# A fused four-block kernel: earlier expert "up" matmuls at the end of block 3, in 19 places that block 3 has left, with pools that wait tile by tile

## The chip, the cores and the metric

The kernel runs on one core of a Trainium2 chip. All data are fp32 apart from the masks. The metric is device time in microseconds (us) for one execution; the median of three runs is taken. The profile is of one execution, with its own time.

Engines: PE is TensorE's matmul and PEld its weight load, DVE is VectorE, ACT is ScalarE, POOL is GpSimd, SP is SyncE, which here issues DMAs.

## The reference

Four blocks follow each other, each on the layer-normalised stream and added back to it:

```python
x = x + L0_attn(layernorm(x))   # block 1: two layers of full attention with an MLP
x = x + L0_ffn(layernorm(x))    # block 2: two layers of windowed attention with a gated MLP
x = x + L1_attn(layernorm(x))   # block 3: windowed and latent attention, mixed by a gate
x = x + L1_ffn(layernorm(x))    # block 4: 64 experts, routed by groups
```

Block 3 has 2 sequences of 1024 positions and width 128, cut into 16 tiles of 128 positions. Its windowed attention has 16 heads of 8 features, its latent attention 4 heads over 64 pooled positions:

```python
local = local_attention(q, k, v)              # window 128
remote = latent(x @ rq, pooled @ rkv) @ rout + rout_b
gate = sigmoid(local @ gl_w + remote @ gr_w)  # per head
out = (gate * local + (1 - gate) * remote) @ out_w + out_b
```

Block 4 computes all 64 experts of 32 hidden features for all 2048 tokens; routing decides what they count for:

```python
scores = softmax(xt @ Wr + br)                # 2048 x 64
# per expert: sort the scores, sum groups of 64 in sorted order,
# keep the best groups over all experts, and mask the scores by them
fs = masked / (masked.sum(-1) + 1e-6)
h = silu(xt @ Wup + bup) * (xt @ Wgate + bgate) * fs[:, :, None]
out = h @ Wdown + fs @ bdown
```

## The kernel before, in words

The blocks run one after another on the core: `stage_a`, `stage_b`, `stage_c`, `stage_d`. In the last two, the order of work on PE, ACT, DVE and POOL is the order in which the program records it (`manual_schedule`), so an instruction waits behind every one that was recorded before it on its engine.

**Block 3 (class `BlockC`).** `prep` (L1139) normalises half a sequence, transposes it to `xT`, and makes queries `qT`, latent queries `rqT`, keys `kT` and values `v`, with a shifted copy `vs`. `score` (L1261), `turn` (L1324), `value` (L1337) and `keep` (L1355) take each tile through scores, softmax, transposed probabilities (`pr`, then `pT`) and values. `latent` (L1395) does the latent attention, `gate` (L1473) the mix of the two and the output projection (transposes L1519, matmuls L1525, added to the stream by `add_tiles`, L517). `both` (L1092) records this in steps; a `Pipe` of "beats" holds work that is due some steps later, and a `beat` records what is due. The last calls of `both`, from L1089, have no new scores to make: they drain what is left. There each step also records two of the sort passes that wait in `front.todo`, unless `self.hold` is set.

**Block 4's front (class `Front`)** runs in those beats too: `tiles` (L1589) normalises a group of finished tiles, transposes it (L1602) into `xTd`, computes router scores (L1608 to L1635), and `turn` (L1643) transposes the scores (L1647) into the layout for sorting, where `sign` (L1657) and sort passes (`sort_pass`, DVE, L1572 and L1573) follow.

**The experts (class `Experts`).** The hidden features are cut into 32 units of two halves each: 64 "up" matmuls (128x128 by 128x512), each followed by a Silu on ACT (L1743) into a place `hid`, and 64 "gate" matmuls of the same size, each multiplied into its `hid`. Most of these products are done by one DVE instruction (L1787); some go through ACT and POOL (L1784, L1785), and eight "late" ones are stored raw by ACT. All these matmuls are line L1734. `up(n)` records n up matmuls and then their n Silus. PSUM tiles are 1024 wide and serve two matmuls each in turn (`bank`, L1082).

Each unit needs a place in SBUF. `new` (L1706) gives them out: the first 10 (`OWN`) in places that block 3 has left, in the pool `own` that outlives it, 19 (`REST`) in a pool of block 4, then two weight tiles, and the last in `xTd` itself, over tokens that every matmul has read by then.

In block 3's end 16 halves are recorded: `up(2)` when the last tile's values are kept (L1390), `up(6)` at the last but one tile's latent output (L1466), `up(2)` after the last gate and `up(2)` three more times in later beats (L1532 to L1534).

**Block 4 (`stage_d`, `route`).** `route` (L1929) runs the remaining sort passes on DVE and, by a running credit, calls `fill` (L1796) between them: one gate product, one more up, and `feed` (L1748), which keeps three gate matmuls ready ahead. When sorted halves have been exchanged by two DMAs (into `r_zab`), a few more passes, group sums (L1981) and a bisection (L2007) follow, then weights for the experts and the down matmuls (L1860) to the output.

PSUM pools (`ps_m`, `ps_c` in block 3, `ps_tr`, `ps_mm`, `ps_d` in block 4) and block 4's SBUF pools (`d1`, `d2`, `dh`) take places that earlier pools have given up. Before, the first use of such a pool waits for all users of the pools whose space it takes.

Of the kernel before, what the change touches and what calls it, by code (L numbers as in the profile page):

```python
# [23 lines left out]
F32 = mybir.dt.float32  # L24
# [5 lines left out]
P = 128  # L30
D = 128
S = 1024
NB = 2
MT = S // P
# [974 lines left out]

def load_c(k, w, I):  # L1010
    nc = k.nc
    k.c_qkv = w.tile([P, 384], F32, name="c_qkv")
    k.c_rq = w.tile([P, 32], F32, name="c_rq")
    k.c_rkv = w.tile([P, 64], F32, name="c_rkv")
    k.c_rout = w.tile([32, D], F32, name="c_rout")
    k.c_out = w.tile([P, D], F32, name="c_out")
    nc.sync.dma_start(k.c_qkv, I["L1_attn_qkv_w"])
    nc.sync.dma_start(k.c_rq, I["L1_attn_rq_w"])
    nc.sync.dma_start(k.c_rkv, I["L1_attn_rkv_w"])
    nc.sync.dma_start(k.c_rout, I["L1_attn_rout_w"])  # L1020
    nc.sync.dma_start(k.c_out, I["L1_attn_out_w"])
# [8 lines left out]
class BlockC:  # L1030
# [61 lines left out]
    def both(self, b=None, m=None, half=None, nxt=None):  # L1092

        on, beat = m is not None, self.pipe.beat
        score, first, second = self.score(b, m, half) if on else [None] * 3
        turn = self.turns and (lambda t=self.turns: self.turn(*t))
        old = self.values
        end, value, keep = [lambda f=f: f(*old) for f in (self.end, self.value, self.keep)] if old else [None] * 3
        if on:
            steps = [[score, end, beat], [beat, value, first], [beat, second, keep], [beat, turn]]  # L1100
        else:
            steps = [[beat, end, value, turn], [beat, keep]]
        for i, now in enumerate(steps):
            for f in now:
                if f:
                    f()
            if nxt and i == 0:
                self.mask(*nxt)
            if not self.hold:
                n = 1 if on else 2  # L1110
                for f in self.front.todo[:n]:
                    f()
                del self.front.todo[:n]
        self.values = self.turns
        self.turns = (b, m, half) if on else None

# [22 lines left out]
    def prep(self, b, j, beats, then=lambda: None):  # L1139
        k, nc, st = self.k, self.k.nc, self.st[b]  # L1140
        t = slice(b * MT + j * 4, b * MT + j * 4 + 4)
        cut = slice(j * 512, (j + 1) * 512)
        new = lambda shape, name: self.p2.tile(shape, F32, tag=name, name=k.name(name))
        if j == 0:
            st["xT"] = self.p1.tile([P, S], F32, tag="xT", name=k.name("xT"))
            st["kT"] = new([P, P + S], "kT")
            for name, rows in (("qT", P), ("rqT", 32)):
                st[name] = self.p5.tile([P, S], F32, tag=name, name=k.name(name))[:rows]
            st["v"], st["vs"] = new([P, MT + 2, 160], "v"), new([P, MT + 1, 160], "vs")
            nc.gpsimd.memset(st["kT"][:, :P], 0.0)  # L1150
            nc.gpsimd.memset(st["v"], 1.0)
            nc.gpsimd.memset(st["vs"][:, 0], 1.0)
# [7 lines left out]
        xT = st["xT"]  # L1160
# [194 lines left out]
    def keep(self, b, m, half):  # L1355
        k, nc, st = self.k, self.k.nc, self.st[b]
        if half == 0:
            st["oT"] = self.p2.tile([P, 2, 4, 64], F32, tag="oT", name=k.name("oT"))
        oT = st["oT"]
        dst, src = oT[:, half].rearrange("p c q -> p (c q)"), st["o"][:, :256]  # L1360
        if self.front.todo or half and (b, m) == (NB - 1, MT - 1):
            nc.scalar.copy(dst, src)
        else:
            nc.vector.tensor_copy(dst, src)  # L1364
        if half == 0:
            return
        local = self.part(b, m, 1, "local")[:, 0, :]
        sel = k.sm("sel", 0, 72).rearrange("p (h n) -> p h n", h=2)

        def rest():  # L1370
            ps = k.bank()
            out = ps[:, :144].rearrange("p (g c d) -> p g c d", c=4, d=9)
            for c in range(4):
                for n in range(2):
                    nc.tensor.matmul(
                        out[n * 64 : n * 64 + 64, :, c, :], oT[:, n, c, :], sel[:, c % 2, :], start=True, stop=True
                    )
            t3 = ps[:, :144].rearrange("p (h d) -> p h d", d=9)
            sums = self.p3.tile([P, 16], F32, tag="sums", name=k.name("sums"))
            nc.vector.reciprocal(sums, t3[:, :, 8])  # L1380
            if m == 0:
                nc.vector.tensor_scalar(sums, sums, k.sm("r1"), None, ALU.mult)
            nc.vector.tensor_tensor(
                local.rearrange("p (h d) -> p h d", d=8), t3[:, :, :8],
                sums[:, :, None].to_broadcast([P, 16, 8]), ALU.mult,
            )
            self.done(b, m)
            if last:
                self.hold = False
                self.ex.up(2)  # L1390

        self.hold = last = (b, m) == (NB - 1, MT - 1)
        self.pipe.later(1 if last else 2, rest, not last, -1 if last else 0)

    def latent(self, b, m):  # L1395
# [55 lines left out]
        def out():  # L1451
            ps = k.bank()
            for u in range(2):
                nc.tensor.matmul(
                    ps[:, u * D : (u + 1) * D], latT[:, u * P : (u + 1) * P], k.c_rout,
                    start=True, stop=True,
                )
            nc.vector.tensor_tensor(
                remote, ps[:, :256].rearrange("p (i d) -> p i d", d=D),
                k.row("c_rout")[:, None, :].to_broadcast([P, 2, D]), ALU.add,  # L1460
            )
            if m == 0:
                self.latent(b, 2)
            self.done(b, m)
            if (b, m) == (NB - 1, MT - 2):
                self.ex.up(6)  # L1466

        self.pipe.chain(
            (1, True, score), (3, False, exp, -1), (2, True, turn), (3, True, value), (2, True, across),
# [3 lines left out]
    def gate(self, b, j):  # L1473
# [48 lines left out]
        def out():  # L1522
            ps = k.bank()
            for i in range(n):
                nc.tensor.matmul(  # L1525
                    ps[:, i * D : (i + 1) * D], mT[:, i * P : (i + 1) * P], k.c_out,
                    start=True, stop=True,
                )
            add_tiles(k, k.xo[:, b * MT + at : b * MT + at + n], ps[:, : n * D])
            self.front.tiles(self, b, at, n)  # L1530
            if last:
                self.ex.up(2)  # L1532
                for beats in (1, 4, 5):
                    self.pipe.later(beats, lambda: self.ex.up(2), False, 1)  # L1534

        beats = (0, 0, 1, 1, 1) if last else (1, 3, 3, 3, 3)
        steps = ((False, products), (False, sums), (False, mix), (True, features), (True, out))
# [151 lines left out]
class Experts:  # L1689
# [1 line left out]

    OWN, REST = 10, 19
    LATE = (26, 29, 32, 35, 58, 60, 62, 64)

    def __init__(self, k, xT, own, wide):
        self.wide = wide
        self.k, self.xT, self.own, self.bank = k, xT, own, None
        self.hid, self.rest, self.raw, self.places = {}, None, {}, []  # L1700
        self.parts = [(tp, h) for tp in range(2) for h in range(NB)]
        self.units = [(tp, h, c) for tp, h in self.parts for c in range(8)]
        halves = [(unit, e) for unit in self.units for e in range(2)]
# [2 lines left out]
    def new(self):  # L1706
        n, k = len(self.hid), self.k
        shape, name = [P, 2, 512], k.name("hid")
        if n < 2 or 8 <= n < self.OWN:
            return self.own.tile(shape, F32, tag=("qT", "rqT")[n % 2], name=name)  # L1710
        if n < self.OWN:
            if n < 6:
                if n % 2 == 0:
                    self.pair = self.own.tile([P, 2048], F32, tag="pr", name=name)
                return self.pair[:, n % 2 * 1024 :][:, :1024].rearrange("p (e t) -> p e t", e=2)
            return self.own.tile(shape, F32, tag="pT", name=name)
        n -= self.OWN
        if n < self.REST:
            return self.rest.tile(shape, F32, tag="hid", name=name)
# [3 lines left out]
        if n == 1:  # L1723
            t = k.wpool.tile([P, NROW], F32, tag="rows", name=name)
            return t[:, :1024].rearrange("p (e t) -> p e t", e=2)

        return self.xT.rearrange("p (b t) -> p b t", b=2)[:, :, :512]

    def matmul(self, unit, e, weights):
# [7 lines left out]
    def up(self, n=1):  # L1737
# [7 lines left out]
            )  # L1745
        del self.ups[:n]

    def feed(self):  # L1748

        while self.gates and len(self.ready) < (3 if self.ups else 4):  # L1750
# [11 lines left out]
    def place(self, k):  # L1762

        if not self.places:
            n, w = len(self.raw), self.wide
            if n == 0:
                t = self.beside.tile([P, 512], F32, name="raw")
            elif n == 1:
                t = w.tile([P, 1024], F32, tag="sc", name="raw_sc")
            elif n == 3:  # L1770
# [25 lines left out]
    def fill(self, n=1):  # L1796


        while n and self.ready:
            now = self.ready.pop(0)  # L1800
            self.gate(*now)
            self.up()
            self.feed()
            n -= not now[0]


def stage_d(k, out, front, ex):
# [2 lines left out]
    nc = k.nc  # L1810
    e = mybir.EngineType
    with ExitStack() as es, k.tc.manual_schedule(engines={e.PE, e.Activation, e.DVE, e.Pool}):
        p1 = es.enter_context(k.tc.tile_pool(name="d1", bufs=1))
        p2 = es.enter_context(k.tc.tile_pool(name="d2", bufs=2))
        ex.rest = es.enter_context(k.tc.tile_pool(name="dh", bufs=ex.REST))
        ex.bank, ex.beside = k.big, p1
        ex.feed()
        fs, rest = route(k, p1, front, ex, ex.fill)
        hid = ex.hid
# [346 lines left out]
def tile_kernel(ctx: ExitStack, tc: tile.TileContext, I, out):  # L2166
    k = K()
# [14 lines left out]
            stage_a(k, b)  # L2182
        stage_b(k, b)
    with ExitStack() as ps:
        psum = lambda n, m: tc.tile_pool(name=n, bufs=m, space=bass.MemoryType.PSUM)
        wcd = ps.enter_context(tc.tile_pool(name="wcd", bufs=1))
        load_d(k, wcd, I)
        front = Front(k, wcd)
# [151 lines left out]
```

## Time and profile before

| | us |
|---|---|
| median of 3 runs (1231.8 to 1233.62) | 1233.22 |
| the profiled execution | 1234.76 |
| its span | 1232.8 |
| PE busy, share of the span | 1091.9 (89%) |
| DVE busy | 866.4 (70%) |
| ACT busy | 618.5 (50%) |
| POOL busy | 483.8 (39%) |

The span lies about so: block 1 to about 330 us, block 2 to 751, block 3 to 985 with its end, in which block 4's front also stands, to 1037, the sort with the experts' matmuls to 1122, and from there bisection, weights and the down matmuls to the end.

How to read the views: a table by stretch gives the busy time of each engine in a stretch of the span, with the TensorE clock that was granted (1.0 is full speed). A list of waits says for each engine and line what ended its idle time, as total, count and longest. The chain that ended last is the work followed back from the last instruction, at each step to what released it. A timeline gives start, duration, engine, line, operation, what is written and read, shape and count, and in square brackets the idle time of the engine before it and what ended it.

### The profile page before, as it was taken

The page shows a single profiled execution, that of the slowest core. Times are in us where ns is not written, and L with a number is a line of the kernel's source. Part 1 is how long each engine was busy: PE and PEld are TensorE (multiplying, and loading weights), DVE is VectorE, ACT ScalarE, POOL GpSimd, SP SyncE. Part 2 cuts the span into 40 slices and gives each one's busy share as a digit, 9 for nine tenths or more (in the row PEclk, how much of TensorE's full clock was granted, in tenths as well). Part 3 has the DMA queues.
Part 4 walks back from the last instruction along what each step waited for, and adds up shares of the span by engine and source line. Part 5 has one row for each costly group of instructions (what it writes and reads, how often), then busy time and mean ns, then how long its engine had stood idle before and what let it go on. Part 6 is the DMA issues. An engine that isn't in the chain of part 4 may idle for free.

```text
span 1232.8 us, 23644 instructions
## 1 busy us (share of the span) xinstructions
PE 1091.9 (89%) x9515; PEld 740.1 (60%) x9547; DVE 866.4 (70%) x1764; ACT 618.5 (50%) x1180; POOL 483.8 (39%) x560
## 2 busy tenths in 40 slices
PE   5999999999778899899899878998999966995799
PEld 2666666665545566666666654665776632442598
DVE  5666675565478767767777743666778999879884
ACT  5555454454355566657556544665666733442100
POOL 1423332224298976766768634222242310200000
PEclk9999999999889999999999988897999988998699
DMA  8100000000011100001000102100000000000000
GB/s 290 34 1 1 1 1 1 1 1 1 1 31 27 23 20 22 23 19 27 19 23 19 23 1 102 27 18 7 2 2 2 2 1 0 1 9 9 1 18 18
DMA packets 23471, 25.56 MB, mean 21 GB/s; under 512 B 6778, under 2 KB 17476, under 8 KB 23108
## 3 DMA queue, kind: packets, MB, share of 16 engines
q1 hardware_dynamic: 23284, 23.81, 7.1%
q8 instruction: 75, 1.23, 0.4%
q10 hardware_dynamic: 80, 0.26, 0.1%
q14 instruction: 32, 0.26, 0.1%
HBM read 13.19 MB, written 1.05 MB: 12 GB/s over the span
## 4 chain that ended last, share of the span: by engine, by line
PE 59%; DVE 26%; ACT 6%; POOL 5%; issue 4%; DMA 0%; DVEq 0%; POOLq 0%; ACTq 0%
PE big L1734 7%; PE bank L410 4%; PE mm L1860 4%; PE s L375 4%; PE bank L965 4%; PE s L730 3%; PE bank L885 3%; DVE r_zab L1572 3%; PE m L1321 3%; PE s L840 2%; PE bank L470 2%; DVE r_zab L1573 2%; PE bank L491 2%; DVE nm L381 2%; PE s L1278 2%
## 5 line engine op out<-in xcount | busy, mean ns | idle before, releaser
L381 DVE TENSOR_REDUCE nm<-s 128x1 f32<-128x1024 f32 x64 | 75.1, 1215 | 51.9 <-PE s L375 51.9
L777 POOL TENSOR_TENSOR t<-raw,tab 128x512 f32<-128x512 f32 x62 | 77.3, 1267 | 74.3 <-DVE raw L768 73.0
L1292 DVE TENSOR_REDUCE nm<-s 128x4 f32<-128x768 f32 x64 | 58.2, 950 | 38.9 <-PE s L1290 33.3
L1734 PE MATMUL big<-xTd,d_gate 128*128 128x512 f32 x128 | 70.6, 646 | 8.6 <-ACT hid L1743 8.0
L739 ACT ACTIVATE sq<-s 128x1024 f32<-128x1024 f32 x32 | 32.8, 1024 | 86.8 <-PE s L730 86.8
L387 ACT ACTIVATE pr<-s,nm 128x1024 f32<-128x1024 f32 x64 | 71.1, 1121 | 7.9 <-DVE nm L381 7.8
L1734 PE MATMUL big<-xTd,d_up 128*128 128x512 f32 x128 | 66.5, 616 | 9.3 <-ACT hid L1743 7.5
L398 PEld LDWEIGHTS bank<-ident,pr 128*128 128x128 f32 x512 | 56.2, 141 | 30.0 <-issue 22.5
L784 POOL TENSOR_TENSOR raw<-raw,tab 128x1024 f32<-128x1024 f32 x31 | 73.2, 2360 | 2.4
L791 POOL TENSOR_TENSOR raw<-raw,t 128x1024 f32<-128x1024 f32 x31 | 73.2, 2362 | 1.7
L410 PE MATMUL bank<-pT,v 128*64 128x128 f32 x1024 | 70.0, 279 | 0.7 <-DVE pT L403 0.2
L401 ACT COPY pT<-bank 128x512 f32<-128x512 f32 x64 | 34.9, 588 | 70.0 <-PE bank L398 70.0
L1743 ACT ACTIVATE hid<-big,cols 128x512 f32<-128x512 f32 x62 | 41.6, 686 | 55.3 <-PE big L1734 55.2
L410 PEld LDWEIGHTS bank<-pT,v 128*64 128x64 f32 x1024 | 55.0, 136 | 22.1 <-issue 10.7
L375 PE MATMUL s<-kk,q 64*128 64x512 f32 x256 | 66.5, 630 | 0.6 <-ACT pr L387 0.5
L398 PE MATMUL bank<-ident,pr 128*128 128x128 f32 x512 | 65.2, 276 | 0.0
L730 PE MATMUL s<-b_wqkv,hT 128*128 128x512 f32 x128 | 63.7, 621 | 1.3 <-ACT hT L697 1.3
L1572 DVE TENSOR_TENSOR r_zab<-r_zab 128x128 f32<-128x128 f32 (+2 forms) x140 | 61.0, 436 | 2.8
L1321 PE MATMUL m<-ident,pr 128*128 128x128 f32 x384 | 58.0, 287 | 5.1 <-DVE oT L1364 2.6
L1573 DVE TENSOR_TENSOR r_zab<-r_zab 128x128 f32<-128x128 f32 (+2 forms) x140 | 55.5, 396 | 0.0
L1860 PE MATMUL mm<-d_down,hid 128*128 128x128 f32 x440 | 53.5, 282 | 0.0
L1860 PEld LDWEIGHTS mm<-d_down,hid 128*128 128x128 f32 x440 | 52.5, 198 | 1.1 <-issue 0.8
(386 smaller groups left out, 2833.8 us busy)
## 6 DMA issues: line engine op xcount, KB each, us to landing
vs<-v SPq DMA_DIRECT2D x60, 130.0 KB, 2.2
b_wqkv<-in_L_ffn_wqkv_dram SPq DMA_DIRECT2D x2, 768.0 KB, 8.9
b_tab<-in_c_xpos_dram SPq DMA_DIRECT2D x1, 1024.0 KB, 9.1
d_up<-in_L_ffn_Wup_dram SPq DMA_DIRECT2D x1, 1024.0 KB
d_gate<-in_L_ffn_Wgate_dram SPq DMA_DIRECT2D x1, 1024.0 KB, 7.0
out_dram<-xo SPq DMA_DIRECT2D x3, 256.0 KB, 2.9
rows<-in_rows_dram SPq DMA_DIRECT2D x1, 760.0 KB, 7.7
vs<-v SPq DMA_DIRECT2D x8, 88.0 KB, 3.6
```

Source lines behind the costliest of these rows:

```text
L375: nc.tensor.matmul(t["s"][h][:, keys], q[rows, qt * P : (qt + 1) * P], kk[rows, keys], start=True, stop=True,)
L381: nc.vector.tensor_reduce(t["nm"][h], t["s"][h], AX.X, ALU.max, negate=True)
L398: nc.tensor.transpose(ps[:, i * P : (i + 1) * P], t["pr", h][:, at : at + P], k.ident)
L410: nc.tensor.matmul(t["u"][h * 64 : h * 64 + 64, :P], v[:, kb, h * 64 : h * 64 + 64], t["pT"][:, h, kb], start=(kb == 0), stop=(kb == MT - 1),)
L730: nc.tensor.matmul(qk[:, cut], lhsT, k.b_wqkv[:, l, cut], start=True, stop=True)
L777: nc.gpsimd.tensor_tensor(t2[:, :, :, a : a + 32], r4[:, :, :, z : z + 32], tab(1)[:, :, None, a : a + 32].to_broadcast([P, 2, 8, 32]), AL ...
L784: nc.gpsimd.tensor_tensor(r4, r4, tab(0)[:, :, None, :].to_broadcast([P, 2, 8, 64]), ALU.mult)
L1321: nc.tensor.transpose(ps[:, c * P : (c + 1) * P], pr[:, c, at : at + P], k.ident)
L1572: nc.vector.tensor_tensor(d[:, :, 0, :], s[:, :, 0, :], far, ALU.max)
L1573: nc.vector.tensor_tensor(d[:, :, 1, :], s[:, :, 0, :], far, ALU.min)
L1734: self.k.nc.tensor.matmul(ps, weights[:, rows], self.xT[:, cut], start=True, stop=True)
L1860: nc.tensor.matmul(sums[part][i], hid[tp, h, c][:, e, cols], k.d_down[:, c + 8 * e, :], start=part == last and c + e == 0, stop=False,)
```

## The change

It has six parts.

1. The five weights of block 3 (`c_qkv`, `c_rq`, `c_rkv`, `c_rout`, `c_out`) become views of one tile `c_w`, whose place later serves the first raw gate product in place of a tile of its own.
2. `prep` takes `xT`, and one tile `kv` for keys, values and shifted values together, from the pool `own`.
3. `OWN` is 19 and `REST` 10: the first 19 units lie where queries, `xT`, `kv` (four units in each), probabilities and transposed probabilities stood.
4. The calls of `up` in `keep`, `latent` and `gate` go. In the draining steps of `both`, `early` records one up (two in the last steps) per step, each matmul with its Silu, until 38 halves are out.
5. `fill` records an up only while more than two are left, and the last two only when half of the gates have been recorded.
6. Block 4's SBUF pools and all PSUM pools of blocks 3 and 4 wait tile by tile (`reuse_waits="tile"`).

```diff
@@ load_c
-    k.c_qkv = w.tile([P, 384], F32, name="c_qkv")
-    k.c_rq = w.tile([P, 32], F32, name="c_rq")
-    k.c_rkv = w.tile([P, 64], F32, name="c_rkv")
-    k.c_rout = w.tile([32, D], F32, name="c_rout")
-    k.c_out = w.tile([P, D], F32, name="c_out")
+    t = w.tile([P, 736], F32, tag="c_w", name="c_w")
+    k.c_qkv, k.c_rq, k.c_rkv = t[:, :384], t[:, 384:416], t[:, 416:480]
+    k.c_rout, k.c_out = t[:32, 480:608], t[:, 608:]
@@ both
                 for f in self.front.todo[:n]:
                     f()
                 del self.front.todo[:n]
+            if not on and not turn:
+                self.ex.early(1 if old or self.hold else 2)
@@ prep
-        new = lambda shape, name: self.p2.tile(shape, F32, tag=name, name=k.name(name))
         if j == 0:
-            st["xT"] = self.p1.tile([P, S], F32, tag="xT", name=k.name("xT"))
-            st["kT"] = new([P, P + S], "kT")
+            st["xT"] = self.p5.tile([P, S], F32, tag="xT", bufs=1, name=k.name("xT"))
+            kv = self.p5.tile([P, 4192], F32, tag="kv", name=k.name("kv"))
+            st["kT"], v, vs = kv[:, : P + S], kv[:, P + S : 2752], kv[:, 2752:]
...
-            st["v"], st["vs"] = new([P, MT + 2, 160], "v"), new([P, MT + 1, 160], "vs")
+            st["v"], st["vs"] = [t.rearrange("p (i d) -> p i d", d=160) for t in (v, vs)]
@@ keep, latent, gate
-                self.ex.up(2)
...
-            if (b, m) == (NB - 1, MT - 2):
-                self.ex.up(6)
...
-            if last:
-                self.ex.up(2)
-                for beats in (1, 4, 5):
-                    self.pipe.later(beats, lambda: self.ex.up(2), False, 1)
@@ Experts
-    OWN, REST = 10, 19
+    OWN, REST = 19, 10
+    PLACES = ("qT", "rqT", "xT", *["kv"] * 4, "qT", "rqT", *["kv"] * 4, *["pr"] * 4, "pT", "pT")
...
-        if n < 2 or 8 <= n < self.OWN:
-            return self.own.tile(shape, F32, tag=("qT", "rqT")[n % 2], name=name)
         if n < self.OWN:
-            if n < 6:
-                if n % 2 == 0:
-                    self.pair = self.own.tile([P, 2048], F32, tag="pr", name=name)
-                return self.pair[:, n % 2 * 1024 :][:, :1024].rearrange("p (e t) -> p e t", e=2)
-            return self.own.tile(shape, F32, tag="pT", name=name)
+            tag = self.PLACES[n]
+            if not self.places_own:
+                size, more = {"kv": (4192, {}), "pr": (2048, {}), "xT": (S, {"bufs": 1})}.get(tag, (S, {}))
+                t = self.own.tile([P, size], F32, tag=tag, name=name, **more)
+                self.places_own = [t[:, i : i + S] for i in range(0, size - S + 1, S)]
+            return self.places_own.pop(0).rearrange("p (e t) -> p e t", e=2)
...
+    def early(self, n):
+
+        for _ in range(n):
+            if len(self.ups) > len(self.gates) - 2 * self.OWN:
+                self.up()
...
-                t = self.beside.tile([P, 512], F32, name="raw")
+                t = self.k.wpool.tile([P, 736], F32, tag="c_w", name="raw_cw")[:, :512]
...
-            self.up()
+            if len(self.ups) > 2 or len(self.gates) <= len(self.units):
+                self.up()
@@ stage_d
-        p1 = es.enter_context(k.tc.tile_pool(name="d1", bufs=1))
-        p2 = es.enter_context(k.tc.tile_pool(name="d2", bufs=2))
-        ex.rest = es.enter_context(k.tc.tile_pool(name="dh", bufs=ex.REST))
-        ex.bank, ex.beside = k.big, p1
+        p1 = es.enter_context(k.tc.tile_pool(name="d1", bufs=1, reuse_waits="tile"))
+        p2 = es.enter_context(k.tc.tile_pool(name="d2", bufs=2, reuse_waits="tile"))
+        ex.rest = es.enter_context(k.tc.tile_pool(name="dh", bufs=ex.REST, reuse_waits="tile"))
+        ex.bank = k.big
@@ tile_kernel
-        psum = lambda n, m: tc.tile_pool(name=n, bufs=m, space=bass.MemoryType.PSUM)
+        psum = lambda n, m: tc.tile_pool(name=n, bufs=m, space=bass.MemoryType.PSUM, reuse_waits="tile")
```

More of the change, by code (lines that the diff above doesn't have):

```diff
@@ L1699, in __init__ @@
         self.k, self.xT, self.own, self.bank = k, xT, own, None
-        self.hid, self.rest, self.raw, self.places = {}, None, {}, []
+        self.hid, self.rest, self.raw, self.places, self.places_own = {}, None, {}, [], []
         self.parts = [(tp, h) for tp in range(2) for h in range(NB)]
@@ L1725, in new @@
             return t[:, :1024].rearrange("p (e t) -> p e t", e=2)
+        assert len(self.gates) <= len(self.units)
         return self.xT.rearrange("p (b t) -> p b t", b=2)[:, :, :512]
```

## The prediction

> **What bounds the kernel now.** I read the page first (PE is busy 89% of the span, DVE 70%), then tables by stretch of the two places that the change touches, block 3's end (985 to 1037 us) and the sort of block 4 (1037 to 1122), then the chain, the waits and the order of work there. In a table by stretch the columns are start:end, length, busy time of PE, PEld, DVE, ACT and POOL (with instructions), granted clock and DMA.
>
> ```profile
> 985.00:995.00 10.00, 8.70 (x48) 5.20 (x48) 9.55 (x29) 3.31 (x6) 0.00 (x0) 1.00 0.00 0
> 995.00:1000.00 5.00, 0.49 (x2) 0.00 (x0) 4.83 (x17) 0.00 (x0) 3.10 (x5) 0.97 0.00 0
> 1000.00:1003.00 3.00, 0.00 (x0) 0.00 (x0) 2.93 (x10) 1.43 (x4) 0.00 (x0) 0.50 0.00 0
> 1020.00:1025.00 5.00, 0.00 (x0) 0.00 (x0) 4.72 (x19) 2.36 (x4) 0.00 (x0) 0.86 0.00 2
> 1040.00:1060.00 20.00, 20.00 (x47) 8.89 (x46) 15.74 (x40) 9.39 (x15) 3.79 (x3) 0.98 0.00 0
> 1080.00:1100.00 20.00, 20.00 (x48) 8.81 (x47) 15.10 (x26) 9.95 (x16) 0.00 (x0) 1.00 0.00 0
> ```
>
> At block 3's end DVE is the bound (9.55 of 10 us) and PE has holes. In the sort it is the reverse: PE is full, DVE has some 4 us free in 20. The chain says so too, and the waits give the size (columns: total, times, longest):
>
> ```profile
> 1037.40 77.42 PE big L1734 x176
> ```
> ```profile
> DVE hid L1787 <- PE big L1734: 14.3, 16, 2.1
> ```
>
> So DVE waits 14.3 us for gate matmuls in the sort: the most that lighter PE work can give there. The matmuls of an up or gate are two records each:
>
> ```profile
> 985.57 1.98 PE L1734 MATMUL big<-xTd,d_up 128*128 128x512 f32 x4
> 990.51 0.71 PE L1525 MATMUL m<-c_out,mT 128*128 128x128 f32 x4 [1.11 <-ACT mT L1520]
> 991.79 3.70 PE L1734 MATMUL big<-xTd,d_up 128*128 128x512 f32 x8
> 1003.00 3.72 PE L1734 MATMUL big<-xTd,d_up 128*128 128x512 f32 x4 [7.51 <-ACT hid L1743]
> 1040.82 1.02 PE L1734 MATMUL big<-xTd,d_gate 128*128 128x512 f32 x2
> 1041.68 1.02 PE L1734 MATMUL big<-xTd,d_up 128*128 128x512 f32 x2
> ```
>
> At full clock one starts every 0.86 us (1040.82, 1041.68); after the idle 7.51 us before 1003.00, at clock 0.56, one takes 1.86 (3.72 for two).
>
> **The change part by part.** The built order has the same number of instructions on each engine; SP's and DVE's orders, and all DMAs on SP's queue, are as before. So costs are waits.
>
> *Ups in block 3's end, 16 halves before, 38 after: +8.6 us.* Before, pairs were recorded as two matmuls and then two Silus (L1743). Now each step records one matmul and its Silu. The two halves of a 1024-wide PSUM tile are written by successive ups, and the built order makes the second wait until ACT has read the first. The handoffs come from this row and its neighbours:
>
> ```profile
> 1032.17 0.69 ACT L1743 ACTIVATE hid<-big,cols 128x512 f32<-128x512 f32 x1 [1.71 <-PE big L1734]
> 1032.91 1.12 PE L1734 MATMUL big<-xTd,d_gate 128*128 128x512 f32 x2 [0.86 <-ACT hid L1743]
> ```
>
> An up that ends at 1032.05 (start 1031.03, 1.02 long) is read at 1032.17, Silu takes 0.69, PE goes on 0.05 later. A pair of halves then takes 1.02+0.12+0.69+0.05+0.86 = 2.74 us, against 1.72. Behind every blocked up stands one matmul group of the chain (L1375, L1431, L1519, L1647, L1448, L1525, L1454, L1602, L1608), behind those groups' ACT copies stand DVE's adds: that is the wait added, and DVE, in unchanged order, is who pays. I walked it with the durations of before. The first up starts at 984.4. Silu's table load (1.28) now precedes the copy of oT L1362, so L1375 ends at 989.95, not 985.65, and L1431 at 990.75, not about 988.35; DVE is +2.4 late. Then a pair each 2.74 us puts L1525's first group at 1000.4, not 990.51 (add L517: 1001.2, not 995.03: +6.2), L1454 at 1006.5 (L1458 +7.1), L1525's second at 1017.1, not 1008.61 (L517: 1017.9, not 1009.51: +8.4). From there DVE has no hole left to be hurt: it is busy 4.72 of 5 us, its eight passes cover exp L1629, and r_zab L1657 comes at 1038.3 instead of 1029.58, the first gate L1787 at 1043.6 instead of 1035.01: +8.6. Bounds: +4 if the handoffs cost only up to the first group and the rest fits the holes (PE idles about 21 us of 52 there, the 22 more halves take 22 x 0.86 = 18.9); +12 if each of 22 steps costs 0.55 us in full. I take the walk, since it has the order itself.
>
> [...]
>
> *Clock: -0.8.* Without the holes PE stays warm. Before, the up and gates between 1035.81 and 1040.82 took 5.0 us for work of 3.4 (4 x 0.86) at full clock. Between 0 and -1.7; DVE is partly the one waited for, so half. [...]
>
> *Sort: -8.1 + 0.3 = -7.8.* Of 48 ups 26 remain, two of them at the end. Up to gate 27 ups and gates still alternate at 0.86, three gates in 5.15 us against DVE's 4.35, so the 6.2 us of DVE waits before 1078 stay. After it the gates come alone, 0.86 per matmul, and DVE needs at least 0.67 each plus its passes. These waits go: 0.23, 2.08, 0.48, 1.41, 0.90, 0.97, 1.03, 0.96 = 8.06:
>
> ```profile
> 1083.15 0.75 DVE L1787 SCALAR_TENSOR_TENSOR hid<-big,cols,hid 128x512 f32<-128x512 f32 x1 [2.08 <-PE big L1734]
> 1093.45 0.75 DVE L1787 SCALAR_TENSOR_TENSOR hid<-big,cols,hid 128x512 f32<-128x512 f32 x1 [1.41 <-PE big L1734]
> ```
>
> What is late next is the exchange of halves before L1968. SP's DMA goes out at 1106.39 and lands 2.9 us later; the five gates that hide it take 6.7 us now and 5 x 0.67 = 3.4 then. Its cover nearly gone, it takes back 0 to 0.6, I say 0.3. Ends: -8.1, and -4 if gates behind ACT's set-aside ones or the five single gates still wait half as long.
>
> *Block 3's start: +2.3.* kT, v and vs now share a tile whose place L982's matmuls read, so POOL's first memset waits for the last of them (about 753.7) instead of DVE L971. And POOL's order changes: L993 and the memsets of d_bdown and d_one come before L1159 and the norm. Before:
>
> ```profile
> 751.22 0.20 POOL L1150 MEMSET kT<- 128x128 f32 x1 [10.36 <-DVE hid L971]
> ...
> 759.07 1.26 POOL L993 TENSOR_TENSOR xo<-xo,xi 128x512 f32<-128x512 f32 x1
> ...
> 760.78 2.05 POOL L1255 TENSOR_TENSOR qm<-qT,small_c 128x512 f32<-128x512 f32 x2
> ```
>
> All the same pieces come after the wait: 753.7 + 0.2 + 1.4 + 1.26 (L993) + 0.2 + 0.35 + 1.25 (L1159) + 3.5 (norm) + 1.25 + 1.06 (first qm) = 764.2, against 761.84. The first scores L1278 began at 761.88 after a wait of 1.83 us for just that qm, and everything on PE is queued behind them; PE is then full (20.00 of 20 at 780 to 800). Ends 0 (later holes take it) and +2.5.
>
> *At nothing.* One weight tile c_w with the same DMAs on SP (landed long before use); the place of raw_cw (read last by L1525, 70 us earlier); 19 units in dead places (their last readers, L1349 and the transposes, end by 984.4); one ordering by tile in place of by pool (D's first gate waits for the last Silu alone; DVE is the later one). Each costs 0 to 0.5 if its cover goes.
>
> **Sum** on the profiled execution, 1234.76 us (span 1232.8 and 1.96 around it): 2.3 + 8.6 - 0.8 - 7.8 = +2.3, so 1237.1. The median of the runs, 1233.22, is 1.5 lower; the forecast is 1235.5. Bisect and down (1122 to the end) move with it unchanged.
>
> **Rivals.**
> - *The ups fall into PE's holes* (ends faster). For it: 21 us of holes for 18.9 of work; against: the built waits. Tail 0 to +4: 1233.2 + 2.3 + 2 - 0.8 - 7.8 = 1228.9; it is faster by more than can be told once block 3's end shifts by less than 3.8. Chance 0.25.
> - *Block 3's start is absorbed*: 1235.5 - 2.3 = 1233.2, no change. For it: DVE has free time until 940; against: the serial chain through PE. 0.17.
> - *Handoffs cost in full*: tail +12: 1235.5 + 3.4 = 1238.9. For it: ACT runs Silus and the chain's copies in one order, and table loads (1.28) part them. 0.2.
> - *The sort's waits do not go* (the change doesn't do what it says there): saved 4: 1235.5 + 3.8 = 1239.3. For it: three ready gates and ACT's set-aside ones limit the run ahead; against: the waits named are all for PE. 0.08.
> - The forecast: 0.3.
>
> **How the numbers follow.** The measurement tells 0.2%, 2.5 us, from no change: faster is below 1230.7, slower above 1235.7. Faster: 0.25 from the first rival. Same: 0.17 plus the lower part of the forecast's own range (1232 to 1239), 0.1: 0.27. Slower: the rest, 0.48. The range reaches from the first rival's 1227 (nearly all of its tail hidden) to 1242 (full handoffs and half the waits left, not both in full).
>
> **What would show.** Right: pairs of ups about 2.7 us apart from 984 to 1040; DVE waiting 2 to 4 us for L1525 and L1454; r_zab L1657 some 9 to 11 us later; the waits DVE on PE after gate 27 gone, about 6 us left; first qm at about 764. Wrong: L1657 shifted by under 5 or over 14, PE still full after gate 27, first scores at 762, or DVE waits at new places in the sort.

## The result, and the profile after

The changed kernel takes 1243.18 us (median of five runs, 1237.89 to 1244.49) against 1233.22; the ratio is 1.0077 with a 95% interval of 1.0055 to 1.0100. Its profiled execution took 1243.0 us with a span of 1241.2. It is slower by 10 us, 1.2 us above the upper end of the range.

The sort is where the change works. The chain's stretch of up and gate matmuls was 77.42 us long and is now

```profile
1052.68 54.92 PE big L1728 x126
```

(line L1734 of before is L1728 here). The waits of DVE for these matmuls, 14.3 us before, are in the list of waits of this stretch:

```profile
DVE hid L1787 <- PE big L1728: 4.5, 7, 0.8
```

The stretches of block 3's end and of the sort, as a table (start:end, length, busy time of PE, PEld, DVE, ACT and POOL, granted clock, DMA):

```profile
985.00:995.00 10.00, 7.67 (x95) 4.57 (x94) 7.92 (x23) 5.57 (x12) 1.73 (x3) 1.00 0.01 3
1000.00:1020.00 20.00, 15.71 (x44) 6.71 (x43) 14.51 (x45) 10.40 (x18) 3.11 (x5) 1.00 0.00 1
...
1060.00:1080.00 20.00, 20.00 (x48) 8.77 (x47) 16.40 (x40) 10.57 (x16) 5.08 (x4) 1.00 0.00 1
1100.00:1120.00 20.00, 16.15 (x35) 5.82 (x34) 19.64 (x32) 1.95 (x3) 0.00 (x0) 1.00 0.10 26
```

From 1100 DVE, not PE, is full: the sort has changed its bound. But from 1000 to 1020, at block 3's end, DVE is busy only 14.51 of 20 us. Before, the same stretch had

```profile
1000.00:1020.00 20.00, 13.15 (x38) 6.33 (x38) 17.49 (x66) 9.68 (x17) 1.19 (x3) 0.84 0.00 1
```

so DVE was busy for 17.49 us there. PE's timeline of the changed kernel shows why:

```profile
998.10 0.38 PE L1516 MATMUL m<-ident,local 128*128 128x128 f32 x2
999.04 1.98 PE L1728 MATMUL big<-xTd,d_up 128*128 128x512 f32 x4 [0.56 <-ACT hid L1737]
1000.86 0.38 PE L1640 MATMUL m<-ident,sc 128*128 128x128 f32 x2
1001.80 1.98 PE L1728 MATMUL big<-xTd,d_up 128*128 128x512 f32 x4 [0.56 <-ACT hid L1737]
1003.62 0.38 PE L1447 MATMUL m<-ident,lat 128*32 128x128 f32 x2
1004.56 1.98 PE L1728 MATMUL big<-xTd,d_up 128*128 128x512 f32 x4 [0.56 <-ACT hid L1737]
1006.38 0.61 PE L1522 MATMUL m<-c_w,mT 128*128 128x128 f32 x4
```

Every group of two halves waits for ACT's Silu, one group each 2.76 us, with one group of the chain behind each. DVE waits for the chain:

```profile
1007.03 0.42 DVE L517 TENSOR_TENSOR xo<-xo,m 128x256 f32<-128x256 f32 x1 [3.84 <-PE m L1522]
...
1046.44 0.48 DVE L1650 TENSOR_SCALAR r_zab<-m,small_c 128x256 f32<-128x256 f32 x1 [2.06 <-PE m L1640]
```

And block 3's start, POOL and then PE of the changed kernel, and last the first scores of before:

```profile
752.71 0.20 POOL L1150 MEMSET kv<- 128x128 f32 x1 [12.37 <-PE bank L982]
...
754.24 1.27 POOL L993 TENSOR_TENSOR xo<-xo,xi 128x512 f32<-128x512 f32 x1
...
762.07 2.05 POOL L1255 TENSOR_TENSOR qm<-qT,small_c 128x512 f32<-128x512 f32 x2
```
```profile
763.17 1.66 PE L1278 MATMUL s<-kv,qm 32*128 32x192 f32 x16 [5.37 <-POOL qm L1255]
...
769.76 1.66 PE L1278 MATMUL s<-kv,qm 32*128 32x192 f32 x16
...
776.73 1.04 PE L1278 MATMUL s<-kv,qm 32*128 32x192 f32 x16
```
```profile
761.88 0.93 PE L1278 MATMUL s<-kT,qm 32*128 32x192 f32 x16 [1.83 <-POOL qm L1255]
```

The first scores come after an idle of 5.37 us in place of 1.83, and take 1.66 us where they took 0.93: the granted clock is 0.50 from 763.1 to 772 and is back at 1.00 from 773 on.

To see where the time goes I cut each profiled execution at five instructions: the end of block 2's last matmuls (L982: 753.71 before, 752.64 after), the end of the last values matmul of block 3 ahead of the first early up (L1349; its rows' start plus duration: 984.50 and 989.71), the start of the last `sign` (r_zab, L1657 of before, L1650 here), of the first gate product (L1787), and of the group sums (L1981, L1982 here). All in us:

| kernel | block 3 | its end, to `sign` | to the first gate | sort, to the group sums |
|---|---|---|---|---|
| before | 230.79 | 45.08 | 5.43 | 86.70 |
| changed | 237.07 | 56.73 | 5.44 | 77.54 |
| difference | +6.28 | +11.65 | +0.01 | -9.16 |

With 0.5 us more from the group sums to the down matmuls and block 2 ending 1.07 earlier this gives +8.2, which is the difference of the two profiled executions (1243.0 - 1234.76). Each stage is from one execution. The end of block 2, whose instructions no edit here changes except for a last add, lies between 748.94 and 754.16 in the twelve profiled executions, so a difference of 2 us between two whole executions can stand ahead of any edit; the stretch of block 3's end repeats much better (45.08, 45.09 and 45.09 in the three with the old pace).

### The profile page after: what moved, and what is told of

Its sections match the earlier page's. It is cut to its first block, busy times and chain, and to the rows that moved or that the text cites. A ratio compares the mean times of both kernels' runs of the same rounds, so it can differ in the third digit from the quotient of the medians.

```text
span 1241.2 us, 23683 instructions
## 1 busy us (share of the span) xinstructions
PE 1099.2 (89%) x9547; PEld 740.2 (60%) x9547; DVE 867.2 (70%) x1764; ACT 620.0 (50%) x1180; POOL 484.6 (39%) x560
## 4 chain that ended last, share of the span: by engine, by line
PE 61%; DVE 22%; ACT 7%; POOL 5%; issue 4%; DMA 1%; DVEq 0%; POOLq 0%; ACTq 0%
PE big L1728 8%; PE bank L410 4%; PE mm L1861 4%; PE s L375 4%; PE bank L965 4%; PE s L730 3%; PE m L1321 3%; PE bank L885 3%; PE s L840 2%; PE bank L470 2%; PE bank L491 2%; DVE nm L381 2%; PE s L1278 2%; PE bank L398 2%; DVE rinv L752 2%
## 5 line engine op out<-in xcount | busy, mean ns | idle before, releaser
L1728 PE MATMUL big<-xTd,d_up 128*128 128x512 f32 x128 | 66.3, 624 | 13.6 <-ACT hid L1737 13.6
L1728 PE MATMUL big<-xTd,d_gate 128*128 128x512 f32 x128 | 68.1, 646 | 8.0 <-DVE hid L1787 6.9
L410 PE MATMUL bank<-pT,v 128*64 128x128 f32 x1024 | 72.5, 286 | 0.7 <-DVE pT L403 0.2
```

The lines of the kernel that those rows point to most:

```text
L410: nc.tensor.matmul(t["u"][h * 64 : h * 64 + 64, :P], v[:, kb, h * 64 : h * 64 + 64], t["pT"][:, h, kb], start=(kb == 0), stop=(kb == MT - 1),)
L1728: self.k.nc.tensor.matmul(ps, weights[:, rows], self.xT[:, cut], start=True, stop=True)
```

## Experiments

All ratios are to the kernel before, run on the same chip. Stages are cut as above.

**The old pace on the new places.** The early ups and the fills are as in before; everything else is the changed kernel.

```diff
-            if not on and not turn:
-                self.ex.early(1 if old or self.hold else 2)
...
+                self.ex.up(2)
...
+            if (b, m) == (NB - 1, MT - 2):
+                self.ex.up(6)
...
-            if len(self.ups) > 2 or len(self.gates) <= len(self.units):
-                self.up()
+            self.up()
```

> The changed kernel with the ups recorded where they were before (2, 6, 2, 2, 2, 2 halves) and one up in every fill; the places, the common tile for keys and values, and the tile-by-tile pools stay. Theory (block 3's start costs 6.0 us: 2.4 for POOL's order and wait, 3.7 for half clock on PE after an idle of 5.4 us; the pace costs 11.9 at block 3's end and returns 9.2 in the sort): 6 us over before, about 1239.2, first scores on PE at about 763 and at half clock, r_zab L1657 six us later than in before. Rival (the whole loss is the pace's; block 3's start is absorbed by 985 us): 1233 to 1234.

Measured: 1238.49 us, ratio 1.0039 (1.0024 to 1.0054). Block 3 takes 233.99, its end 45.09, the sort 85.10. So the pace makes the whole +11.65 at block 3's end (45.09 without it, 45.08 before) and 7.56 of the 9.16 saved in the sort (the other 1.60 came with the places and the pools; which of them gave it isn't separated), and the new places cost on their own: 5 us in the median, +3.2 in the profiled execution's block 3. That execution is the fastest of its four, and where the median loses the rest isn't shown. That its block 3 is 3 us shorter than the changed kernel's, with the same instructions in the same order, is the clock: in both the first scores come 10.5 us after L982 and take 1.66, but the next stretch ran at 0.93 of full clock here (first line) and at 0.74 there (second line):

```profile
765.00:780.00 15.00, 13.25 (x123) 7.78 (x115) 10.99 (x23) 8.31 (x19) 2.71 (x5) 0.93 0.39 92
```
```profile
765.00:780.00 15.00, 14.26 (x102) 8.34 (x104) 9.49 (x20) 8.30 (x18) 0.81 (x2) 0.74 0.32 72
```

The clock was 0.50 up to 767 here, and up to 772 there.

**Block 3's start, POOL without the add.**

```diff
-                later(1, lambda: nc.gpsimd.tensor_tensor(k.xo[:, cut], k.xo[:, cut], k.xi[:, cut], ALU.add))
+                eng = nc.vector if (b, j) == (NB - 1, 1) else nc.gpsimd
+                later(1, lambda: eng.tensor_tensor(k.xo[:, cut], k.xo[:, cut], k.xi[:, cut], ALU.add))
...
-        ex = Experts(k, front.xT, ps.enter_context(tc.tile_pool(name="c5", bufs=2)), wcd)
+        ex = Experts(k, front.xT, ps.enter_context(tc.tile_pool(name="c5", bufs=2, reuse_waits="tile")), wcd)
```

> The changed kernel with two edits at block 3's start alone: block 2's last add to the stream (L993) on DVE, which idles there, and the pool of the common places waiting tile by tile, so that POOL has neither the add nor the wait for L982 ahead of its norm in block 3. Theory: first query masks qm at about 760 (relative to an end of L982 at 752.6), an idle of PE ahead of the first scores under 2.5 us, scores at full clock (0.93 for 16 where the changed kernel has 1.66); 6 to 7 us under the changed kernel, 1236 to 1237. Rival (the start's delay is absorbed later): within 1 us of the changed kernel, 1242 to 1243.

Measured: 1241.85 us, ratio 1.0066 (1.0051 to 1.0081): a miss. The wait moved. POOL now stood behind the d_bdown memset, which waits for the add on DVE:

```profile
755.01 0.31 POOL L1552 MEMSET d_bdown<- 128x256 f32 x1 [12.43 <-DVE xo L994]
```
```profile
762.57 0.93 PE L1279 MATMUL s<-kv,qm 32*128 32x192 f32 x16 [4.06 <-POOL qm L1256]
763.44 1.46 PE L1291 MATMUL s<-mask_c,identb 128*128 128x384 bf16 x4
```

The idle was still 4.06 us; the first scores were fast, the matmuls right behind them at half clock (1.46 for 0.82). Block 3 takes 234.40, 2.67 less than in the changed kernel, but its end takes 58.36, 1.63 more: there the granted clock fell to between 0.50 and 0.72 from 990.9 to 999.6, behind an idle of PE of 2.12 us (the four groups there took 2.65, 1.08, 1.90 and 3.29 us, in the changed kernel 1.98, 0.66, 1.07 and 1.96). So part of the start did come back and was lost again later.

**Pairs of ups.**

```diff
-        for _ in range(n):
+        self.due += n
+        while self.due >= 2:
+            self.due -= 2
             if len(self.ups) > len(self.gates) - 2 * self.OWN:
-                self.up()
+                self.up(2)
```

> The changed kernel with each two halves of an early up recorded as two matmuls and then two Silus, in every second step: same matmuls, Silus and places, without the wait of a second half for the first half's Silu. Theory (that wait sets block 3's end): ups of a pair 0.86 apart, r_zab L1657 late by about 4 us (2 to 6) in place of 11.9, the time 6 to 9 us under the changed kernel, 1234 to 1237. Rival (the amount of work moved, 22 more matmuls of 0.86 and 22 more Silus of 0.69 in front of the chain's own, sets it): L1657 within 3 us of the changed kernel's, 1240 to 1243.

Measured: 1232.01 us, ratio 0.9983 (0.9971 to 0.9994), 11 us under the changed kernel and better than I had expected. Block 3's end takes 46.23: 1.15 more than before, where I had expected 2 to 6 more, with the same 22 more matmuls and Silus in it as the changed kernel's 56.73. The sort takes 79.30. The rival falls: the work fits the holes, and recording the halves one by one, in one tile, was the cost. The run with different PSUM tiles below parts the wait from the pace. PE's timeline:

```profile
996.41 0.38 PE L1516 MATMUL m<-ident,local 128*128 128x128 f32 x2
996.63 1.88 PE L1729 MATMUL big<-xTd,d_up 128*128 128x512 f32 x4
998.35 0.38 PE L1640 MATMUL m<-ident,sc 128*128 128x128 f32 x2
998.57 1.88 PE L1729 MATMUL big<-xTd,d_up 128*128 128x512 f32 x4
1000.29 0.38 PE L1447 MATMUL m<-ident,lat 128*32 128x128 f32 x2
```

No bracket, no wait: one pair and one group of the chain each 1.94 us, not 2.76.

**PE kept busy ahead of the first scores.** Six matmuls whose results nobody reads.

```diff
+        idle = self.k.bank()
+        for _ in range(6):
+            self.k.nc.tensor.matmul(idle, self.k.ident, self.st[0]["xT"][:, :512], start=True, stop=True)
         self.mask(*tiles[0])
```

> The changed kernel with six useless matmuls (identity by 512 columns, 0.86 us each at full clock) on PE between the values L1177 and the first scores of block 3, where it idles 5.4 us; POOL's order and waits stay. Theory (3.7 of the 6.0 us at the start are half clock): first scores start where they did, run at full clock (0.93 for 16), and the time is 3 to 4 us under the changed kernel, 1239 to 1240. Rival (the clock is not what is lost; all 6 are order and wait): 1242 to 1244.

Measured: 1237.83 us, ratio 1.0036 (1.0021 to 1.0051), 5.4 under the changed kernel and faster than either expectation; its runs spread widely, 1232.86 to 1241.53.

```profile
759.10 5.32 PE L1073 MATMUL m<-xT,ident 128*128 128x512 f32 x12
764.63 0.93 PE L1281 MATMUL s<-kv,qm 32*128 32x192 f32 x16 [0.22 <-POOL qm L1258]
```

The first scores start just as late as in the changed kernel (10.53 us after L982's end) and run at full clock, and block 3 takes 233.36 in place of 237.07. Useless work won 3.7 us in block 3 here: that much of the 6.28 was half clock. What is left against before, 2.57, is order and wait: the first scores are 10.53 - 8.17 = 2.36 later. The profiled execution is the slowest of the ten (1241.53). The five shortest (1232.86 to 1236.83) had a mean granted clock of 0.968 to 0.971, the five longest 0.960 to 0.964; where in the kernel the shorter ones gained isn't shown, so the 5.4 us of the median are explained only as far as the 3.7.

**Successive ups in different PSUM tiles**, one up and its Silu per step as in the changed kernel.

```diff
-        turn = itertools.cycle(("s0", "s1"))
-
         def bank():
-            for tag in turn:
-                wide = self.k.ps_c.tile([P, 1024], F32, tag=tag, name=self.k.name("big"))
-                yield wide[:, :512]
-                yield wide[:, 512:]
+            while True:
+                wide = [
+                    self.k.ps_c.tile([P, 1024], F32, tag=tag, name=self.k.name("big")) for tag in ("s0", "s1")
+                ]
+                for half in (slice(0, 512), slice(512, 1024)):
+                    for t in wide:
+                        yield t[:, half]
```

> The changed kernel, one up and its Silu per step as there, but successive ups go to the two 1024-wide PSUM tiles in turn (first half of one, first half of the other, second halves), so that an up waits for the Silu of the one before last instead of the last. Theory (the wait inside a tile is the cost, not the pace of one by one): the same gain as with pairs, r_zab L1657 late by 1 to 3 us over before against the start of the stretch (11.7 in the changed kernel), the time 1231 to 1235. Rival (recording a Silu right behind each up puts the Silus ahead of the chain's copies on ACT, and that costs): at most half of the 11 us comes back, 1237 to 1243.

Measured: 1232.79 us, ratio 0.9990 (0.9980 to 1.0001). Block 3's end takes 48.57, 8.2 less than in the changed kernel and 3.5 more than before, a little over what I expected; the sort takes 77.22. So most of the cost, 8.2 of 11.65 us, was not the steady pace of one up per step but which tile the next up writes. The 2.3 us over the run with pairs stay with the pace; they are not followed further.

**Block 3's start again, with the two memsets on DVE too** (in addition to the edits of the second experiment).

```diff
-    nc.gpsimd.memset(k.d_bdown, 0.0)
+    nc.vector.memset(k.d_bdown, 0.0)
...
-    nc.gpsimd.memset(k.d_one, 1.0)
+    nc.vector.memset(k.d_one, 1.0)
```

> The run with the add L993 on DVE and the pool waiting by tile, and in addition the two memsets of d_bdown and d_one on DVE: in that run POOL stood behind the d_bdown memset, which waited for the add until 755.0 and kept the first qm at 762.5. Theory: POOL's norm starts at the end of DVE's statistics (about 752), the first qm ends about 758, PE goes on to the scores without an idle of over 1 us and at full clock; block 3 up to its end is 6 us shorter than in the changed kernel, 1236 to 1238. Rival (the start's delay is absorbed later): 1241 to 1243.

Measured: 1240.52 us, ratio 1.0060 (1.0043 to 1.0077), between the two expectations. The start did what I expected:

```profile
759.73 0.93 PE L1279 MATMUL s<-kv,qm 32*128 32x192 f32 x16 [0.72 <-POOL qm L1256]
...
988.77 3.22 PE L1729 MATMUL big<-xTd,d_up 128*128 128x512 f32 x4 [2.12 <-ACT hid L1738]
991.92 1.04 PE L1376 MATMUL m<-small_c,oT 128*64 128x36 f32 x16
```

Block 3 takes 231.75, 5.3 less. But its end now takes 58.30, 1.6 more than in the changed kernel: after the 2.12 us in which PE waits for the first Silu and its table load, the two halves took 3.22 here and 1.98 there, and the group behind them 1.04 for 0.66, which makes the 1.6. The changed kernel's row is

```profile
992.88 1.98 PE L1728 MATMUL big<-xTd,d_up 128*128 128x512 f32 x4 [2.12 <-ACT hid L1737]
```

In this execution the clock was 0.60 behind the wait (988.7 to 992.1), in that of the changed kernel 1.00 (992.8 to 995).

**Both mends**, pairs and start.

> Both mends at once: pairs of ups, and block 3's start with add and memsets on DVE and the pool waiting by tile. Theory (the two costs are independent and the sort's saving of 7 to 9 us stays): 1224 to 1228, faster than before by about 0.6%. Rival (DVE or PE sets block 3's length anyway once the start is mended): 1231 to 1233.

Measured: 1224.39 us (1221.51 to 1228.14), ratio 0.9935 (0.9910 to 0.9959): it beats both kernels, as the theory had it. Block 3 takes 230.64, its end 46.21, the sort 78.23; against before that is -0.15, +1.13 and -8.47. The first scores come 5.87 us after L982, 2.3 earlier than in before, and block 3 is no shorter for it: ahead of before's point something else bounds it, and which engine that is was not looked for.

**The kernel before, with the add and the memsets on DVE.**

```diff
-                later(1, lambda: nc.gpsimd.tensor_tensor(k.xo[:, cut], k.xo[:, cut], k.xi[:, cut], ALU.add))
+                eng = nc.vector if (b, j) == (NB - 1, 1) else nc.gpsimd
+                later(1, lambda: eng.tensor_tensor(k.xo[:, cut], k.xo[:, cut], k.xi[:, cut], ALU.add))
...
-    nc.gpsimd.memset(k.d_bdown, 0.0)
+    nc.vector.memset(k.d_bdown, 0.0)
...
-    nc.gpsimd.memset(k.d_one, 1.0)
+    nc.vector.memset(k.d_one, 1.0)
```

> The kernel before with its add L993 of block 2's last tiles and the memsets of d_bdown and d_one on DVE, nothing else. In before POOL ran them at 759.1 to 760.8, right ahead of the first qm. Theory (POOL sets block 3's start there too): first scores about 1.7 us earlier, the time 1231 to 1232. Rival (absorbed later): 1233.

Measured: 1231.99 us, ratio 0.9986 (0.9976 to 0.9997). The time is as the theory had it, but the first scores came only 0.25 us earlier (7.92 after L982 in place of 8.17), so the step that I named did not happen and the time fits it by luck: of the 2.8 us between the two profiled executions, 2.3 lie ahead of L982's end, and where the median's 1.9 come from isn't shown. The mended start is worth little by itself. It is worth 7.6 us together with pairs (1232.01 to 1224.39), where it takes away what the new places had cost (block 3 goes from 237.10 to 230.64), but only 2.7 in the changed kernel (1243.18 to 1240.52) and 2.3 with alternating tiles (1232.79 to 1230.47, below). Why it pays so differently is open.

**34 early halves in place of 38.**

```diff
-            if len(self.ups) > len(self.gates) - 2 * self.OWN:
+            if len(self.ups) > len(self.gates) - 34:
```

> The changed kernel with 34 early halves in place of 38; the other four are recorded in the sort's fills. Open so far: why the stretch from the last values to r_zab L1657 takes 11.65 us more than before, where the prediction's walk had 8.6. Theory (the last early ups stand ahead of the transposes L1640 on PE, behind two table loads and at half clock, and DVE waits 2.06 us for L1640): that stretch is 2 to 3 us shorter than in the changed kernel (54 to 55 against 56.73), and the sort gives back 2 to 3.5 us less, 1242 to 1244 in all. Rival (the excess is spread over all pairs): the stretch is at most 1 us shorter, 1244 to 1246.

Measured: 1242.68 us, ratio 1.0073 (1.0058 to 1.0088). Block 3's end takes 54.60, 2.13 less than in the changed kernel, and the sort 79.73, 2.19 more, so the total hardly moves (1242.68 for 1243.18). The transposes L1640 now wait for DVE and not the other way round:

```profile
1039.99 0.66 PE L1640 MATMUL m<-ident,sc 128*128 128x128 f32 x2 [3.14 <-DVE sc L1628]
```

In the changed kernel they stood behind ups that waited for Silus behind exp's and Silu's table loads, and that ran at about half clock (0.54 from 1042.5 to 1046.2):

```profile
1038.25 1.28 ACT L1622 ACT_TABLE_LOAD   x1
...
1039.97 1.28 ACT L1737 ACT_TABLE_LOAD   x1
```
```profile
1042.59 3.60 PE L1728 MATMUL big<-xTd,d_up 128*128 128x512 f32 x4 [2.32 <-ACT hid L1737]
1046.02 0.38 PE L1640 MATMUL m<-ident,sc 128*128 128x128 f32 x2
```

**Alternating tiles with the mended start.**

> Ups to the two tiles in turn, one per step, with block 3's start mended as in the run with pairs. Theory (costs of start and stretch are independent): 5 to 8 us under the run with alternating tiles alone, 1225 to 1228, and about as fast as pairs with the mended start (1224.4). Rival (the gain of pairs with the start was the clock's phase): 1229 to 1232.

Measured: 1230.47 us (1226.96 to 1231.62), ratio 0.9971 (0.9960 to 0.9982), between the two expectations. Its profiled stages are as the theory has them (block 3 230.51, its end 48.66, the sort 77.25), but most of its executions were longer than the profiled one, by 2 to 3 us. Why is open.

## Why the prediction was wrong

The sign of the sum was right, and so were the signs of its parts; two of them were too small, and they add. The profiled execution came out 5.9 us over the sum's 1237.1: 4.0 from block 3's start, 3.05 from its end, less 0.56 in the sort and 0.6 outside these stages.

- **"Block 3's start: +2.3"** is the step that failed first: it measured +6.28. The walk of POOL itself was right: the first scores came 2.36 us later against L982's end. What the term left out is that the longer idle of PE, 5.37 us in place of 1.83, costs the clock as well: a granted clock of 0.50 for the first scores and what follows, 3.7 us in the profiled execution by the run with useless matmuls, and between 0.6 and 3.7 over the five profiled executions that share this start (block 3 takes 237.07, 233.99, 237.10, 234.37 and 234.25 in them, and 233.36 with those matmuls). The upper end that I gave, +2.5, was the order's alone. I had priced the clock at block 3's end, where I took the change only to warm PE, and not where it made a new idle. Behind an idle of the same length (5.37 and 5.34 us) the clock came back at 773 in one execution, 9.8 us after the first scores began, and at 767 in another, 3.0 after; what sets the moment isn't shown. Behind the idle of 2.12 us at block 3's end 1.6 us were lost in two executions (those of the two runs with a mended start and single ups) and nothing in that of the changed kernel, and no run here separates the cause.
- **"Ups in block 3's end: +8.6"** was the right mechanism (the run with different PSUM tiles takes back 8.2 of it), undersized: 11.65 measured, near the upper end of 12. The period was 2.76 for 2.74, the first add 6.8 late for 6.2 (12.0 less the 5.2 by which the stretch began later), the second 9.5 for 8.4. Of the 3.05 us missing, 2.13 are one place, shown by the run with 34 halves: I let DVE's passes cover exp and walked L1640 straight behind, but the last early ups stood in front of it with two table loads and half clock ahead of them. The other 0.9 was there by the second add and is not put down to a place.
- **"Clock: -0.8" and "Sort: -8.1 + 0.3 = -7.8"**, together -8.6, were 9.16. The waits after gate 27 fell from 8.06 to 0.2, those before it from 6.2 to 4.3 (the 1.55 at the fifth gate went whole: that was the clock's term, near its end of -1.7 rather than half; the term counts four matmuls between 1035.81 and 1040.82, where the trace has three, 2.6 us of work, so that its end should have been -2.4). The exchange that I named as next waited 1.07 us, not 0 to 0.6:

```profile
1120.71 1.23 DVE L1969 SCALAR_TENSOR_TENSOR r_zab<-r_zab 128x1024 f32<-128x1024 f32 x1 [1.07 <-DMA r_zab<-r_zab]
```

- **The rivals.** "Handoffs cost in full" (+12) has the number of block 3's end, but partly by luck: 2.13 of the 11.65 are the one place before L1640, and not 22 equal steps. Added to the start's clock it left the range. "The ups fall into PE's holes" fell for this kernel, and the run with pairs shows that it holds as soon as the wait inside a tile goes: 1.15 us for 22 more matmuls. "The start is absorbed" fell: the 6.28 of block 3's start stood undiminished at its end, and the run with both mends got 6.5 of block 3 back. What held of it is that scores earlier than in before bring nothing.
- **The range** took each unknown by itself; both stretches can lose the clock, in the same direction, and the range did not hold both.
- "At nothing": the tile-by-tile waits, the common weight tile and the place of raw_cw show no cost: the old pace on the new places has 45.09 for 45.08 at block 3's end, and its sort, where raw_cw is used, takes 85.10 for 86.70.

## What to carry to other kernels

Before moving matmuls into PE's holes, follow which PSUM tile each one writes and who reads that tile last: with two halves in a tile, a reader recorded between them put ACT's whole turnaround on PE here (2.76 us a pair in place of 1.94), and with it everything that is queued behind. Where a change makes a new idle on PE, price the clock with it and not only the idle (here 0.6 to 3.7 us behind an idle of about 5.4). And when two buffers are joined or moved, read the first writer's waits and the order on its engine again: a memset that waits can put a chain of small work on POOL behind it (here the first scores came 2.36 us later).

## What I had not expected of the hardware

Six useless matmuls made the kernel faster by 5.4 us in the median (1243.18 to 1237.83). Executions of the same order differ by 3 us in block 3, with the granted clock at 0.74 or 0.93 behind the same idle. The runs of one kernel can spread by much more than those of before (1231.8 to 1233.62): 1232.86 to 1241.53 in the run with useless matmuls, in which that idle is filled. So that idle alone doesn't make the spread, and its cause is open.
